# Queuing the steps that weigh batch 6's projections one product later

## The chip, the cores and the metric

The kernel runs on one core of a Trainium2 chip. The metric is the device time of one execution in microseconds (us), taken as the median of several runs. A core has engines with queues of their own: TensorE (PE, matrix products), VectorE (DVE), ScalarE (ACT), GpSimd (POOL) and SyncE (SP), which here only issues DMA transfers. Each engine takes its own instructions in order, and waits on semaphores for the others.

## The reference

The input x has 8 batches of 256 tokens with 1024 features, in float32. Every batch is first multiplied by one of eight 1024x1024 matrices, chosen by an index. The result, here called y, goes through a linear layer ("the base") and a mixture of eight low-rank updates:

```
y      = einsum('bsi,boi->bso', x, weight[ids])
base   = y @ base_W.T + base_b
probs  = softmax(y @ router_W.T + router_b)         # 15 choices per token
p, i   = top_k(probs, 8)
w      = sum of p by expert_map[i]                  # 8 experts
h      = einsum('btd,erd->bter', y, A)              # 8 experts x rank 16 = 128 values
lora   = einsum('bter,eor->bto', h * w, B) * 2
out    = x + base + lora
```

"Weighing the projections" is the product h * w for one batch, with the softmax, the choice of eight and the sum by expert that give w.

## The kernel before

**Two phases.** The first phase loops over the eight batches and computes y for each. It also projects a finished batch: `project(b, ph)` (line 129) multiplies y by the 128 columns of A and the 15 columns of the router at once (line 136). It returns six closures: `logits`, `softmax`, `top`, two of `route_to`, and `weigh`. `logits` reads the PSUM tile; the others work on small tiles in one large buffer named `late`; `weigh` multiplies h by w and transposes the result in 32x32 blocks through `flip` (line 244). `turn(b, hw)` (line 250) then makes 16 ScalarE copies (line 255) that put the blocks in place in `hwT0` or `hwT1`: the first holds batches 0 to 3, the second batches 4 to 7.

At the end of the first phase batch 6 is projected and its `logits` run; its other five closures are left in `steps`, which the second phase keeps as `steps_of` (line 568).

**The second phase** computes base and update for two groups of four batches (g = 0, 1). A group's 2x2 block product is itself written as seven outer products (`seven`, line 742), and each of them (`product`, line 597) again as seven blocks on PE, so that the base is done by a fast scheme in two levels. Counted over both groups, `here` numbers the outer products from 0 to 13; `n` counts within a group. A product works in three PSUM tiles:

- `pa`: a11 b11; then s2 t2 added; then s3 t3 added; then a22 t4 added
- `pc`: s1 t1; then s4 b22 added
- `pb`: a12 b21

In order the seven blocks are: `pa`, `pc`, `pa`, `pb`, `pa`, `pc`, `pa`. After each block, VectorE (or ScalarE where the base's bias is added, line 618) reads the tile as it stands: `take` copies it into the result quarter with a summand, `plus` adds it to a quarter (line 609). Since `pa` is added to in place, PE's next block into `pa` has to wait until the reader of the state before is done. Some products (n = 1, 3, 4, 6) also add the low-rank update to four of their blocks, by a matmul of the tiles `hwT` and `up` for each half (line 588); such a block takes PE longer.

**The order of the work is written out by hand** in this phase: PE, VectorE, ScalarE and SP take the instructions in the order in which the program issues them. Small VectorE work is fitted between the blocks through two queues, `soon` and `later`:

```
def fill(n):
    for _ in range(n):
        if soon or later:
            soon.popleft()() if soon else later.popleft()[1]()
```

Ahead of each of the seven blocks stands `gap(k)`, k = 0 to 6. It first runs the functions listed for that gap in `gaps[k]`, and then `fill(2)`. So the "third gap" is `gap(2)`, ahead of the block s2 t2. At the end of a product `fill(len(soon))` empties `soon` whatever its length, and `later` is worked off as far as it holds results of earlier quarters. What is queued in this way:

- the differences that the next product needs as its t1 to t4 (line 229; `advance`, put at the front of `soon`): two in gap 0, one in gap 3, one in gap 4
- the updates of y between the products (`first_terms` in product 0, `outer` in products 2 and 3; line 732)
- the residual add of x to a finished quarter and its output DMA (lines 703 and 704, in `later`)
- the weighing of batch 6 (`steps_of`) and of batch 7 (behind product 1)

After product 1 the kernel issues `turn` for batch 6 on ScalarE, projects batch 7 on PE and queues its steps; `turn` for batch 7 follows product 2.

DMA loads of the weights run through SP: `load_left` (line 206) fetches a product's seven block sums as two tiles, `left_raw` (line 209, 1024 KB) and `left_sum` (line 213, 768 KB). In gap 5 of a product those for the product after the next are issued. The quarters of x for the residual are loaded by `load_x` (line 694) in the gaps 0 to 3 of a product that ends in results. SP is a queue as well: a load that stands behind an output goes no earlier than that output.

Of the kernel before, what the change touches and what calls it, by code (L numbers as in the profile page):

```python
# [28 lines left out]
def kernel(  # L29
# [176 lines left out]
    def load_left(n):  # L206

        ra = wpool.tile([P, NS, 4 * P], F32, name="wt")
        nc.sync.dma_start(
            ra.rearrange("p s f -> p (s f)"), left_raw[n].rearrange("p s f -> p (s f)")  # L210
        )
        su = wpool.tile([P, NS, 3 * P], F32, name="wt")
        nc.sync.dma_start(
            su.rearrange("p s f -> p (s f)"), left_sum[n].rearrange("p s f -> p (s f)")
        )
        return ra, su

    def differences(right):

        b11, b12, b21, b22 = right[:, 0, 0], right[:, 0, 1], right[:, 1, 0], right[:, 1, 1]  # L220
        t = {}

        def minus(n, of, less):
            def run():
                t[n] = tpool.tile([P, 2 * S], F32, name="tt").rearrange(
                    "p (k o) -> p k o", k=2
                )
                x, y = (t[v] if isinstance(v, int) else v for v in (of, less))
                nc.vector.tensor_sub(t[n], x, y)
                return t[n]  # L230

            return run

        return [minus(1, b12, b11), minus(2, b22, 1), minus(3, b22, b12), minus(4, b21, 2)]
# [11 lines left out]
    def run(steps, n=None):  # L246
        for _ in range(len(steps) if n is None else min(n, len(steps))):
            steps.popleft()()

    def turn(b, hw):  # L250

        to = hwTs[b // GB][:, b % GB // 2, b % 2].rearrange("p (j a t) -> p j a t", j=NTT, a=4)
        return deque(
            (
                lambda a=a, r=r: nc.scalar.copy(  # L255
                    to[32 * r : 32 * r + 32, :, a, :],
                    hw[32 * a : 32 * a + 32, :, ts(r, 32)],
                )
            )
            for r in range(4)  # L260
            for a in range(4)
        )
# [282 lines left out]
    with ExitStack() as phase:  # L545
# [21 lines left out]
        soon, later = deque(), deque()  # L567
        steps_of = steps
# [110 lines left out]
        for g in range(B // GB):  # L679
            y, hw = yv[g], hwTs[g]  # L680
            end = g == B // GB - 1
            b11, b12, b21, b22 = y[:, 0, 0], y[:, 0, 1], y[:, 1, 0], y[:, 1, 1]
            u = mpool.tile([P, 2, 2, 2, S], F32, name="u")
            t2 = mpool.tile([P, 2, 2, 2, S], F32, name="t2")
            xs = {}

            def number(oh, th, i, j):
                return ((g * 2 + oh) * 2 + th) * 4 + 2 * i + j

            def load_x(*r):  # L690
                nonlocal loaded
                xs[r] = places_x[loaded % len(places_x)]
                loaded += 1
                nc.sync.dma_start(xs[r].rearrange("p m t -> p (m t)"), xr[number(*r)])

            def finish(oh, th):


                def done(i, j, q):
                    x, n = xs[oh, th, i, j], number(oh, th, i, j)  # L700

                    def run():
                        add(q, q, x)
                        nc.sync.dma_start(outq[n], q.rearrange("p m t -> p (m t)"))

                    later.append((q, run))

                return done

            def joint(i, j, q):  # L710


                def run():
                    add(q, v[:, i, j], q)

                soon.append(lambda: add(u[:, i, j], u[:, i, j], q))
                later.append((q, run))
                finish(1, 1)(i, j, q)

            def last(i, j, q):  # L720
                if (i, j) == (1, 0):
                    for mi in range(2):
                        nc.sync.dma_start(outq[number(1, 0, 1, 0), :, ts(mi, S)], q[:, mi])
                else:
                    finish(1, 0)(i, j, q)

            def at(t):
                return lambda i, j: t[:, i, j]

            def update(dst, x, z, quarters=((0, 0), (0, 1), (1, 0), (1, 1))):  # L730
                return [
                    (lambda i=i, j=j: sub(dst[:, i, j], x[:, i, j], z[:, i, j]))
                    for i, j in quarters
                ]

            def first_terms(*quarters):

                for q in quarters:
                    soon.extend(update(b11, b12, b11, [q]))
                    soon.extend(update(t2, b22, b11, [q]))  # L740

            seven = [

                (b11, 0, at(u), nothing),
                (b21, at(u), fresh, finish(0, 0), 0, hw[:, 0]),
                (t2, at(u), at(u), nothing),
                (b11, at(u), at(v), nothing, 1, hw[:, 1]),
                (b22, at(v), fresh, finish(0, 1), 2, hw[:, 1]),
                (b12, KH, fresh, joint),
                (b21, at(u), fresh, last if end else finish(1, 0), 1, hw[:, 0]),  # L750
            ]
            result_of = {1: (0, 0), 4: (0, 1), 5: (1, 1), 6: (1, 0)}

            outer = {2: update(b12, b22, b12), 3: update(b21, b21, t2)}

            for n, (right, base, into, done, *up_hw) in enumerate(seven):
                here = g * len(seven) + n
                gaps = {k: [] for k in range(7)}

                if n + 1 < len(seven):  # L760
                    follows = seven[n + 1][0]
                else:
                    follows = None if end else yv[g + 1][:, 0, 0]
                steps = [] if follows is None else differences(follows)
                nexts = []


                def advance(n, steps=steps, nexts=nexts):
                    def run():
                        soon.extendleft(  # L770
                            (lambda s=s: nexts.append(s())) for s in reversed(steps[n])
                        )

                    return run


                steps = [steps[:2], steps[2:3], steps[3:]]
                for k, m in ((0, 0), (3, 1), (4, 2)):
                    gaps[k].append(advance(m, steps))
                if n == 0:  # L780
                    gaps[1].append(lambda: first_terms((0, 0), (0, 1)))
                    gaps[4].append(lambda: first_terms((1, 0)))
                    gaps[6].append(lambda: first_terms((1, 1)))
                    if here == 0:
                        gaps[6].append(lambda: soon.extend(steps_of))
                elif n in outer:
                    gaps[1].append(lambda n=n: soon.extend(outer[n]))
                if n in result_of:
                    for k, ij in enumerate([(0, 0), (1, 1), (0, 1), (1, 0)]):
                        gaps[k].append(lambda r=result_of[n] + ij: load_x(*r))  # L790
                if end and n == 6:

                    r = (1, 0, 1, 0)
                    gaps[5].append(
                        lambda: soon.append(lambda: add(u[:, 1, 0], u[:, 1, 0], xs[r]))
                    )
                if here == 0:
                    for k, count in enumerate((0, 1, 1, 4, 4, 4, 2)):
                        gaps[k].append(lambda count=count: run(behind, count))
                if here + 2 < len(lefts):  # L800

                    def fetch(m=here + 2):
                        left[m] = load_left(lefts[m])

                    gaps[5].append(fetch)
                product(
                    left.pop(here), terms, right, base, into, done, gaps, *up_hw,
                    *([None] * (2 - len(up_hw))), end and n == 6
                )
                terms = nexts  # L810
                if here == 1:
                    run(turn(*waiting))

                    ph = ps_e.tile([P, 2, S], F32, name="pe")
                    steps, waiting = project(B - 1, ph)
                    soon.extend(steps)
                elif here == 2:
                    run(turn(*waiting))
# [65 lines left out]
```

## Time and profile before

| | |
|---|---|
| median of 3 runs | 435.79 us (435.49 to 436.15) |
| the profiled execution | 435.38 us |
| its span, first to last instruction | 433.6 us |
| TensorE busy | 426.8 us (98%) |
| VectorE busy | 328.9 us (76%) |
| ScalarE busy | 166.9 us (39%) |
| moved through DMA | 106.05 MB |

The span is what the profiler sees between the first and the last instruction; the time of the execution is a little longer. A busy share is an average over the span. In the rows of a timeline the first number is the start in us from the span's start, the second the duration, then engine, line, operation, and output <- inputs; a bracket gives the idle time before the row and what ended it. In the chain, the first number is the time at which a piece of the chain begins, the second how long it lasts. VectorE's rows may overlap a little: a row of 128x512 lasts 0.68 us and the next starts 0.60 us after it.

### The profile page before, as it was taken

To read this page: it belongs to the slowest core of one execution; us is meant where nothing else is said; L and a number is where in the kernel's file an instruction comes from. 1 tells how busy PE (TensorE), PEld (TensorE's weight loads), DVE (VectorE), ACT (ScalarE), POOL (GpSimd) and SP (SyncE) were. 2 spreads that over 40 slices of the span, in tenths; PEclk is the share of its full clock that TensorE was granted. 3 is DMA by queue.
4 is the path that set the end of the run, shared out by engine and by line. 5 is a ranking of instruction groups with operands and counts; after the bars stand their busy time and mean duration, and the time that the engine had idled before them with its cause. 6 is when DMAs were issued, how large, how long until landed. Compare 5 with 4: busy or idle time off the path is not lost.

```text
span 433.6 us, 4931 instructions
## 1 busy us (share of the span) xinstructions
PE 426.8 (98%) x1642; PEld 293.4 (68%) x1642; DVE 328.9 (76%) x556; ACT 166.9 (39%) x458; POOL 0.7 (0%) x6
## 2 busy tenths in 40 slices
PE   8999999999999999999999899999999999999997
PEld 5344554644646446454468798888888888888886
DVE  0799999986878898998786766946597858745595
ACT  1029287866659657686748500300201100000200
POOL 0000000000000000000000000000000000000000
PEclk9999999999999999999999999999999999999999
DMA  7996998968777797782859365522958725912843
GB/s 278 415 349 251 370 334 280 331 204 299 246 261 242 284 359 260 284 277 89 290 222 379 150 206 208 187 105 97 379 213 278 278 76 198 393 53 68 296 158 134
DMA packets 32779, 106.05 MB, mean 245 GB/s; under 512 B 3058, under 2 KB 6898, under 8 KB 29554
## 3 DMA queue, kind: packets, MB, share of 16 engines
q1 hardware_dynamic: 32610, 105.21, 66.8%
q10 hardware_dynamic: 144, 0.52, 0.3%
q8 instruction: 13, 0.21, 0.2%
q14 instruction: 12, 0.10, 0.1%
HBM read 84.49 MB, written 21.23 MB: 244 GB/s over the span
## 4 chain that ended last, share of the span: by engine, by line
PE 95%; DMA 2%; DVE 2%; SPq 1%; issue 0%; DVEq 0%
PE pa L290 24%; PE pa L579 21%; PE pc L290 13%; PE pc L579 11%; PE pb L290 7%; PE ph L136 6%; PE pb L579 6%; PE pc L588 3%; DMA wt<-in_wq_dram 2%; PE pb L588 2%; PE pa L588 1%; PE pe L136 1%; PE pe L579 1%; SPq L359 0%; DMA ids_sb<-in_ids_dram 0%
## 5 line engine op out<-in xcount | busy, mean ns | idle before, releaser
L308 ACT COPY y<-late 32x256 f32<-32x256 f32 x256 | 103.0, 402 | 41.9 <-DVE late L244 38.9
L579 PE MATMUL pa<-tt,wt 128*128 128x256 f32 x324 | 78.2, 380 | 1.6 <-DVE q L609 1.6
L579 PEld LDWEIGHTS pa<-tt,wt 128*128 128x128 f32 x324 | 61.2, 190 | 10.8 <-DVE q L609 2.0
L290 PE MATMUL pa<-wt,x 128*128 128x512 f32 x128 | 57.7, 593 | 0.4 <-DMA wt<-in_wq_dram 0.3
L290 PE MATMUL pa<-wt,tt 128*128 128x512 f32 x120 | 54.0, 593 | 0.0
L618 ACT ACTIVATE q<-pa,bb 128x256 f32<-128x256 f32 x12 | 5.0, 471 | 105.0 <-PE pa L579 104.0
L290 PEld LDWEIGHTS pa<-wt,x 128*128 128x128 f32 x128 | 24.2, 190 | 31.1 <-issue 30.2
L290 PEld LDWEIGHTS pa<-wt,tt 128*128 128x128 f32 x120 | 22.3, 190 | 26.2 <-issue 25.9
L255 ACT COPY hwT<-late 32x64 f32<-32x64 f32 x128 | 31.1, 243 | 10.6 <-DVE late L244 9.1
L136 PEld LDWEIGHTS ph<-late,y 128*128 128x128 f32 x224 | 28.4, 189 | 3.3 <-issue 3.3
L290 PE MATMUL pb<-wt,x 128*128 128x512 f32 x64 | 29.0, 594 | 0.4 <-DMA wt<-in_wq_dram 0.4
L290 PE MATMUL pc<-wt,x 128*128 128x512 f32 x64 | 28.9, 594 | 0.0
L290 PE MATMUL pc<-wt,tt 128*128 128x512 f32 x64 | 28.8, 592 | 0.0
L136 PE MATMUL ph<-late,y 128*128 128x143 f32 x224 | 28.6, 284 | 0.0
L579 PE MATMUL pc<-tt,wt 128*128 128x256 f32 x112 | 27.8, 379 | 0.0
L405 DVE TENSOR_TENSOR wt<-wt 128x2048 f32<-128x2048 f32 (+1 forms) x9 | 18.4, 2046 | 7.9 <-PE pa L290 5.5
L579 PE MATMUL pb<-y,wt 128*128 128x256 f32 x96 | 24.0, 379 | 0.0
L579 PE MATMUL pc<-y,wt 128*128 128x256 f32 x96 | 24.0, 379 | 0.0
L579 PEld LDWEIGHTS pc<-tt,wt 128*128 128x128 f32 x112 | 21.3, 190 | 2.9
L290 PEld LDWEIGHTS pb<-wt,x 128*128 128x128 f32 x64 | 12.1, 190 | 16.1 <-issue 14.3
L290 PEld LDWEIGHTS pc<-wt,x 128*128 128x128 f32 x64 | 12.1, 190 | 15.5 <-issue 14.8
L290 PEld LDWEIGHTS pc<-wt,tt 128*128 128x128 f32 x64 | 12.1, 190 | 15.3 <-issue 14.6
(118 smaller groups left out, 548.3 us busy)
## 6 DMA issues: line engine op xcount, KB each, us to landing
wt<-in_wq_dram SPq DMA_DIRECT2D x28, 1024.0 KB, 5.7
wt<-left_raw SPq DMA_DIRECT2D x14, 1024.0 KB, 5.7
wt<-left_sum SPq DMA_DIRECT2D x14, 768.0 KB, 7.6
out_dram<-q SPq DMA_DIRECT2D x31, 256.0 KB, 2.3
x<-in_xq_dram SPq DMA_DIRECT2D x7, 1024.0 KB, 6.9
late<-in_xr_dram SPq DMA_DIRECT2D x20, 256.0 KB, 6.6
wt<-in_wq_dram SPq DMA_DIRECT2D x8, 512.0 KB, 7.4
spare<-in_bq_dram SPq DMA_DIRECT2D x4, 1024.0 KB, 5.1
```

What stands on the lines that cost most here:

```text
L136: nc.tensor.matmul(ph[:, j, : ER + N], lhsT=y[:, k // KH, th, k % KH // 2, bi, k % 2, ts(j, P)], rhs=ar_sb[:, k, :], start=(j == order[0] ...
L255: lambda a=a, r=r: nc.scalar.copy(to[32 * r : 32 * r + 32, :, a, :], hw[32 * a : 32 * a + 32, :, ts(r, 32)],)
L290: nc.tensor.matmul(acc, lhsT=right[:, k, :], rhs=left[:, k, :], start=(first and k == 0), stop=(k == KH - 1), skip_group_check=True,)
L308: lambda a=a, r=r: nc.scalar.copy(y[32 * r : 32 * r + 32, :, :, a, :], m[32 * a : 32 * a + 32, :, :, r, :])
L405: nc.vector.tensor_add(q["s1"][:, h], q["a21"][:, h], q["a22"][:, h])
L579: nc.tensor.matmul(acc[mi][:, mi, :], lhsT=left[:, 2 * k + mi, :], rhs=right[:, k, :], start=(first and k == 0 and (mi == 0 or acc[0] is n ...
L588: nc.tensor.matmul(acc[mi][:, mi, :], lhsT=up[:, ts(mi, P)], rhs=hw, start=False, stop=True, skip_group_check=True,)
L618: nc.scalar.activation(dst[:, mi], acc[mi][:, mi], AF.Identity, bias=bb[:, c : c + 1])
```

## The change

The five closures left from batch 6 (`steps_of`) are appended to `soon` in gap 2 of outer product 1, where they were appended in gap 6 of outer product 0. In both kernels they are taken out by the same `fill`.

```diff
                     gaps[1].append(lambda: first_terms((0, 0), (0, 1)))
                     gaps[4].append(lambda: first_terms((1, 0)))
                     gaps[6].append(lambda: first_terms((1, 1)))
-                    if here == 0:
-                        gaps[6].append(lambda: soon.extend(steps_of))
                 elif n in outer:
                     gaps[1].append(lambda n=n: soon.extend(outer[n]))
+                if here == 1:
+                    gaps[2].append(lambda: soon.extend(steps_of))
                 if n in result_of:
```

The instructions of PE, ScalarE and GpSimd keep their order. On VectorE the rows from line 160 to the transpose of line 244, which stood together between the last update of y (line 732) and the first difference for product 2 (line 229), come apart:

- softmax and top (lines 160 to 179) stand behind the take of quarter (1,1) from `pc`, ahead of the take of (0,1) from `pa`
- the two route steps (lines 186 and 189) stand each behind one difference, ahead of the adds to (0,0) and to (1,1)
- the weighing and its transpose (lines 194 and 244) stand behind the add to (1,1), ahead of the first residual add

The residual adds from `later` come one place later as well: the first, ahead of the add to (1,1) before, now stands behind it; the second, ahead of the add to (0,1) before, now stands behind it. On SP the first output of product 1 follows the two weight loads of gap 5, where it stood ahead of them.

## The prediction

> **What bounds the kernel now.** I read the page first (shares and the chain), then who TensorE (PE) waited for, then the chain in order of time around the moved steps, then VectorE's (DVE) timeline there, last the DMA in stretches.
>
> ```profile
> span 433.6 us, 4931 instructions
> PE 426.8 (98%) x1642; PEld 293.4 (68%) x1642; DVE 328.9 (76%) x556; ACT 166.9 (39%) x458; POOL 0.7 (0%) x6
> PE 95%; DMA 2%; DVE 2%; SPq 1%; issue 0%; DVEq 0%
> ...
> PE pa L579 <- DVE q L609: 1.6, 1, 1.6
> PE pb L427 <- POOL ident masks.py:199: 1.4, 1, 1.4
> ```
>
> PE is busy for 426.8 of 433.6 us and is 95% of the chain that ended last. After the start-up it has one wait worth naming: once, 1.6 us, on the DVE instruction of line 609. The chain shows what stands in front of it:
>
> ```profile
> 236.34 1.74 PE pc L579 x8
> ...
> 240.19 0.10 DVE late L160
> ...
> 243.19 0.45 DVE late L244
> 243.64 0.59 DVE tt L229
> ...
> 244.93 0.69 DVE q L609
> 245.62 0.04 issue
> 245.66 1.99 PE pa L579 x8
> 247.66 0.86 PE pb L579 x4
> ```
>
> From 238.2 to 245.6 us the chain runs through DVE; everywhere else around here it runs through PE. The stretch 240.19 to 243.64 is exactly the moved steps (lines 160 to 244). DVE's timeline gives the order behind it:
>
> ```profile
> 240.11 0.18 DVE L160 TENSOR_REDUCE late<-late 128x2 f32<-128x30 f32 x1
> ...
> 243.19 0.45 DVE L244 STREAM_TRANSPOSE late<-late 128x256 f32<-128x256 f32 x1
> 243.56 0.65 DVE L229 TENSOR_TENSOR tt<-t 128x512 f32<-128x512 f32 x1
> 244.32 0.69 DVE L229 TENSOR_TENSOR tt<-t,tt 128x512 f32<-128x512 f32 x1
> 244.93 0.68 DVE L609 TENSOR_TENSOR q<-pa,u 128x512 f32<-128x512 f32 x1
> 245.53 0.68 DVE L609 TENSOR_TENSOR q<-pc,u 128x512 f32<-128x512 f32 x1
> 247.69 0.69 DVE L609 TENSOR_TENSOR q<-pa,u 128x512 f32<-128x512 f32 x1 [1.49 <-PE pa L579]
> ```
>
> The reader sees a queue: softmax to transpose, two differences, then the take of quarter (0,0) out of `pa`. PE's third block of product 1 accumulates into that same `pa` and may not start before the take has read it. PE's own rows have `pc` finished at 243.52 + 0.59 = 244.11 and the third block released at 245.66, just behind the take's end (244.93 + 0.68 = 245.61):
>
> ```profile
> 243.52 0.59 PE L588 MATMUL pc<-hwT,up 128*128 128x256 f32 x2
> 245.66 0.70 PE L579 MATMUL pa<-tt,wt 128*128 128x256 f32 x2 [1.55 <-DVE q L609]
> ```
>
> **The change part by part.**
>
> *Added and removed instructions:* none. Five closures (softmax, top, two route steps, weigh with its transpose) move on DVE from the end of product 0 into product 1. PE's and ScalarE's (ACT) orders stay as they are; on SyncE's (SP) queue one line trades places.
>
> *What leaves the end of product 0.* From the start at 240.11 to the start of the next row at 243.56: 3.45 us of DVE. With it gone, the differences start at 240.11 and 240.87 (0.76 apart, as now), and the take of (0,0) could start 0.61 later, at 241.48. But it also needs PE's first block, which starts at 239.63 and lasts 1.89: 241.52, plus the 0.04 that DVE needs after PE's end (247.65 to 247.69). So the take runs from 241.56 to 242.24. PE reaches its third block at 241.36 + 2.59 = 243.95 (2.59 is a block with the small rank-16 products: 247.66 to 250.25 in the chain). The take is 1.71 us early, so the wait is gone whole, not shortened.
>
> *What that is worth.* Idle time 1.55 (244.11 to 245.66), and the block that restarts costs 1.99 where one in the flow costs 1.73 in the chain: 0.26 more. Sum 1.81 us. The nearest rows bound it: at least 1.55 if the restart were paid anyway, at most the 1.95 that the weight loads sat idle. I take 1.81.
>
> *Where the 3.45 us go.* Each gap queues steps and runs two closures. Softmax and top run in the third gap, behind the take of `pc`; a difference and a route step in each of the fourth and fifth; weigh in the sixth. My timeline, PE without the wait, DVE pitches 0.60 for a 128x512 row:
> - PE: third block 243.95, `pb` 245.68, fifth block (`s3`) 248.27, `pc` again 250.00, last (`a22`) 252.59, projection of batch 7 from 255.18.
> - DVE: take of (1,1) from `pc` 244.15, then softmax and top (240.11 to 241.60: 1.49) from 244.75 to 246.24. Take of (0,1) out of `pa` starts 246.24; PE had it ready at 245.88. It is 0.36 late and ends at 246.92. PE's fifth block needs it at 248.27: 1.35 us spare.
> - Difference 246.84, route step (241.60 to 242.12: 0.52) to 247.97; `pb` is ready at 248.47, so the add to (0,0) is on time and ends 249.16. Difference 249.07, route step (0.62) to 250.29; the add of `pa` to (1,1) is ready at 250.20, so 0.09 late, done 250.97; PE's last block needs it at 252.59: 1.62 spare. (The two differences are read only in product 2.)
> - Weigh and transpose (242.74 to 243.56: 0.82) to about 251.7, one residual add to 252.3, the add of `pc` to (0,1) on time at 252.79. Two residual adds to 254.6; the take of (1,0) waits for PE at 255.38.
>
> So the 3.45 us fit into idle time that DVE has now: 1.49 before its row at 247.69, 1.30 before 250.28, 1.10 before 254.60 (idle on DVE in front of PE). Cost on the path: 0.
>
> *Who waits for the later transpose.* The 16 ACT copies of batch 6 (line 255) start at 243.67 now and would start near 251.8 and end near 256 (4.06 us). The next ACT work is the exponential of batch 7 at 264.16 now, some 262.4 then; 6 us of cover. These copies fill the half of `hwT1` that only the second group reads. The `hw0`, `w`, `kept` places are rewritten by batch 7's steps behind them on the same engine.
>
> *SP.* The residual add of (0,0) falls behind the sixth gap, so the two loads of the weights for product 3 (1024 + 768 KB) are queued ahead of its output, not behind it. They stand behind that output today and go at 252.65; they would go when SP is done with the x loads, at 233.61 + 0.92 = 234.5. The DMA engines are then nearly full:
>
> ```profile
> 236.00:240.00 4.00, 4.00 (x20) 3.54 (x19) 3.60 (x7) 3.65 (x10) 0.00 (x0) 1.00 0.99 413
> 240.00:244.00 4.00, 4.00 (x20) 3.27 (x18) 3.69 (x18) 0.99 (x4) 0.00 (x0) 1.00 0.67 253
> 244.00:248.00 4.00, 2.45 (x12) 2.08 (x12) 2.41 (x5) 3.57 (x15) 0.00 (x0) 1.00 0.00 0
> ```
>
> The transfers in flight end near 242.5; 1.83 MB more at 413 GB/s take 4.4 us, to 247, into a stretch that is empty now. Even if everything ended then, the x loads are first read at 251.5 and product 2's weights from 259.1. Cost 0, with 4.5 us of cover; the gain of earlier weights is 0 too, since PE never waits for them. The output of (0,0) goes out 0.2 us after its add, near 252.5; its tile is wanted again in product 4.
>
> *Sum.* The profiled execution took 435.38 us (span 433.6), 0.41 below the median 435.79. 435.38 - 1.81 = 433.57 for an execution like it; for a median of runs 435.79 - 1.81 = 433.98. From 245.66 on the chain is PE to the end, so the 1.81 us are not lost again unless one of the covers above fails.
>
> [...] By the rows, PE's blocks keep 1.73 us whatever DVE does, and DVE is busy 11.85 of 17.30 us between 239.8 and 257.1. [...]
>
> **The rivals.**
> 1. *The wait moves.* Softmax and top sit before the take of (0,1), the routes before the add to (1,1). If these run later than laid out by more than 1.35 or 1.62 us, PE's fifth or last block waits. For: the two are the only rows that my layout has late (0.36, 0.09). Against: all durations come from this very chain. With a wait of 0.3 to 0.9 us in place of 1.81: 434.3 to 434.9.
> 2. *DVE has no room:* the 3.45 us displace takes one for one and PE loses at the fifth and seventh blocks what it gained at the third. It would need the idle 1.49 + 1.30 + 1.10 not to be usable. Against: those rows wait for PE's results, not the reverse, and DVE is idle 5.45 of the 17.30 us. Same as before, 435.8. [...]
> 3. *Slower: the early weights.* 1.83 MB enter the DMA queue 18 us earlier, among x loads that take 10 us to land now. A residual add that waits for its x holds everything behind it on DVE: one more add, two residual adds, the take of (1,0), two differences, and then product 2's take of (0,0), seven rows of 0.60 to 0.76, some 4.5 us. PE reads past that take at product 2's third block, near 262.5, so it starts to cost once x lands after about 257.4, ten us behind the 247 above. To be slower than before by 0.9 it takes 257.4 + 1.8 + 0.9, near 260: 436.7. Against: they are issued ahead of the new loads.
>
> **How the numbers follow.** Forecast 0.86; rival 1 0.06; rival 2 0.05; rival 3 0.03. A measurement of this kernel tells about 0.2% (0.9 us) from no change. Half of rival 1 is faster by more than that. Faster 0.86 + 0.03 = 0.89; same 0.03 + 0.05 = 0.08; slower 0.03. The runs before spread from 435.49 to 436.15, so -0.30 and +0.36; the gain lies between 1.55 and 1.95. Low 435.49 - 1.95 = 433.5, high 436.15 - 1.55 = 434.6; I take 433.3 to 434.9, which takes in rival 1. The likeliest is 434.0.
>
> **What would show it.** Right: PE's line "waits for DVE q L609, 1.6" is gone; the span is near 431.8; the rows of lines 160 to 179 stand behind the take of `pc`, and the copies of line 255 start near 252; the weight loads for product 3 are issued near 234.5; PE idle between 240 and 257 is under 0.2. Wrong: a wait of PE on DVE at the fifth or last block of product 1, a wait on DMA in product 2, or a residual add (line 703) that waits for its x load.

## The result and the profile after

The changed kernel takes 434.02 us (median of 6 runs, 433.51 to 434.73) against 435.79 us (6 runs, 435.49 to 436.15): 0.9959 of the time before, 95% interval 0.9946 to 0.9972, that is 1.8 us less.

The page of the changed kernel, and from the list of whom TensorE waited for, all that is left:

```profile
span 432.3 us, 4927 instructions
PE 426.6 (99%) x1642; PEld 293.6 (68%) x1642; DVE 328.6 (76%) x556; ACT 167.0 (39%) x458; POOL 0.7 (0%) x6
PE 96%; DMA 2%; SPq 1%; issue 0%; DVE 0%
...
PE pb L427 <- POOL ident masks.py:199: 1.4, 1, 1.4
PE pb L290 <- DMA wt<-in_wq_dram: 1.0, 2, 0.6
PE pa L290 <- DMA wt<-in_wq_dram: 0.4, 1, 0.4
```

The wait of TensorE (PE) on the take of line 609 is gone. Busy times of PE and VectorE (DVE) are what they were, so no work went away. What is left are waits in the first microseconds, and these differ between profiled executions: 0.4 + 0.3 us on the first weights before, 1.0 + 0.4 here. Product 1 starts later in this profile, at 240.15 and not at 239.63. To compare the kernels I take the stretch from the start of product 1's first block to the end of the span: 433.6 - 239.63 = 193.97 before, 432.3 - 240.15 = 192.15 after, 1.82 us less. Both spans are given to 0.1 us, so such differences are good to about 0.1.

The chain of the changed kernel in order of time (start, length, what) runs through PE alone:

```profile
236.86 1.73 PE pc L579 x8
238.59 3.45 PE pa L579 x16
242.04 0.86 PE pc L579 x4
...
244.63 1.73 PE pa L579 x8
246.36 0.86 PE pb L579 x4
```

The third block, which cost 1.99 us behind a wait before, takes 1.73. VectorE's timeline in the same place:

```profile
240.63 0.68 DVE L229 TENSOR_TENSOR tt<-t 128x512 f32<-128x512 f32 x1
241.42 0.69 DVE L229 TENSOR_TENSOR tt<-t,tt 128x512 f32<-128x512 f32 x1
242.08 0.69 DVE L609 TENSOR_TENSOR q<-pa,u 128x512 f32<-128x512 f32 x1
244.67 0.69 DVE L609 TENSOR_TENSOR q<-pc,u 128x512 f32<-128x512 f32 x1 [1.90 <-PE pc L588]
245.28 0.17 DVE L160 TENSOR_REDUCE late<-late 128x2 f32<-128x30 f32 x1
...
246.54 0.19 DVE L179 TENSOR_TENSOR late<-late 128x30 f32<-128x30 f32 x1
246.65 0.68 DVE L609 TENSOR_TENSOR q<-pa,u 128x512 f32<-128x512 f32 x1
...
248.99 0.69 DVE L609 TENSOR_TENSOR q<-pb,q 128x512 f32<-128x512 f32 x1 [0.55 <-PE pb L588]
```

The take of (0,0) now starts when PE's first block is done, and PE reaches its third block 1.70 us after that take ends (242.77 to 244.47). VectorE then idles 1.90 us for `pc`, and only behind it come softmax and top. The take of (0,1) at 246.65 is the row that could become the next wait; it ends at 247.33, and PE wants it at 248.79, so its spare is 1.46 us.

### The profile page after: what moved, and what is told of

It is laid out like the page before. It is cut to its first block, busy times and chain, and to the rows that moved or that the text cites. A ratio compares the mean times of both kernels' runs of the same rounds, so it can differ in the third digit from the quotient of the medians.

```text
span 432.3 us, 4927 instructions
## 1 busy us (share of the span) xinstructions
PE 426.6 (99%) x1642; PEld 293.6 (68%) x1642; DVE 328.6 (76%) x556; ACT 167.0 (39%) x458; POOL 0.7 (0%) x6
## 4 chain that ended last, share of the span: by engine, by line
PE 96%; DMA 2%; SPq 1%; issue 0%; DVE 0%
PE pa L290 24%; PE pa L579 22%; PE pc L290 13%; PE pc L579 11%; PE pb L290 7%; PE ph L136 6%; PE pb L579 6%; PE pc L588 3%; DMA wt<-in_wq_dram 2%; PE pb L588 2%; PE pa L588 1%; PE pe L136 1%; PE pe L579 1%; SPq L359 0%; DMA ids_sb<-in_ids_dram 0%
```

## The experiments

Each was compared with the kernel before on the same chip, which took 435.57 us beside the first four kernels, 435.80 beside the next four and 435.70 beside the last. "Stretch" is product 1's start to the end of the span, as above.

**How much may stay ahead of the take of (0,0)?** Two kernels put a part of the steps back at the end of product 0.

```diff
+                    if here == 0:
+                        gaps[6].append(lambda: soon.extend(steps_of[:2]))
...
-                    gaps[2].append(lambda: soon.extend(steps_of))
+                    gaps[2].append(lambda: soon.extend(steps_of[2:]))
```

> Softmax and top (1.49 us of VectorE) go back to the end of product 0, the other 1.96 us of the 3.45 stay in product 1. Threshold theory: the take of (0,0) has 1.7 us to spare in the changed kernel, 1.49 fits, so TensorE still does not wait at the third block of product 1 and the median is that of the changed kernel, 434.0 (product 1's start to the end 192.15 us). Rival, each microsecond ahead of the take costs its share: 434.0 + 1.81 * 1.49/3.45 = 434.8.

Measured: 433.91 us (433.67 to 434.31), ratio 0.9963 (0.9949 to 0.9976); stretch 432.5 - 240.35 = 192.15, the same as the changed kernel's. PE has no wait. The first row of softmax, and the rows up to the take of (0,0) and the one behind it:

```profile
240.83 0.17 DVE L160 TENSOR_REDUCE late<-late 128x2 f32<-128x30 f32 x1
...
242.20 0.68 DVE L229 TENSOR_TENSOR tt<-t 128x512 f32<-128x512 f32 x1
242.99 0.69 DVE L229 TENSOR_TENSOR tt<-t,tt 128x512 f32<-128x512 f32 x1
243.60 0.69 DVE L609 TENSOR_TENSOR q<-pa,u 128x512 f32<-128x512 f32 x1
244.87 0.69 DVE L609 TENSOR_TENSOR q<-pc,u 128x512 f32<-128x512 f32 x1 [0.58 <-PE pc L588]
```

The take of (0,0) ends at 244.29, 0.38 us before PE is due at 240.35 + 4.32 = 244.67. The proportional theory (434.8) falls.

With `[:4]` and `[4:]` in place of `[:2]` and `[2:]`:

> All but the weighing and its transpose go back: 3.45 - 0.82 = 2.63 us ahead of the take of (0,0). Threshold theory: the take ends 0.82 earlier than before, at product 1's start + 5.16; TensorE wants it at + 4.32, so a wait of about 0.73 and a restart 0.26 dearer, about 1.0 us over the changed kernel: 435.0. Rival, proportional: 434.0 + 1.81 * 2.63/3.45 = 435.4.

Measured: 434.76 us (434.31 to 435.88), ratio 0.9984 (0.9975 to 0.9993); stretch 432.9 - 239.87 = 193.03, 0.88 over the changed kernel. From VectorE's timeline, then PE's:

```profile
240.35 0.18 DVE L160 TENSOR_REDUCE late<-late 128x2 f32<-128x30 f32 x1
...
242.86 0.68 DVE L229 TENSOR_TENSOR tt<-t 128x512 f32<-128x512 f32 x1
...
244.25 0.69 DVE L609 TENSOR_TENSOR q<-pa,u 128x512 f32<-128x512 f32 x1
```

```profile
239.87 1.89 PE L579 MATMUL pa<-y,wt 128*128 128x256 f32 x8
...
244.99 1.99 PE L579 MATMUL pa<-tt,wt 128*128 128x256 f32 x8 [0.64 <-DVE q L609]
```

The wait is back with 0.64 us, in its old place. So the cost is a threshold. With 1.37 us of the steps ahead (240.83 to 242.20) nothing is lost, with 2.51 us (240.35 to 242.86) 0.88, with the 3.45 us of the kernel before 1.82: between the last two, 0.94 us more of the steps costs 0.94 us more. The threshold itself lies near the spare of 1.70 us; no kernel was run just above it. The restarted block is 0.1 dearer in its own length again (1.99, not 1.89).

**Is there room behind it?** Softmax and top, whose results do not change when they are repeated, run twice or three times in the third gap.

```diff
-                    gaps[2].append(lambda: soon.extend(steps_of))
+                    gaps[2].append(
+                        lambda: soon.extend(
+                            [lambda: [s() for s in steps_of[:2] * 1 + steps_of[:1]]] + steps_of[1:]
+                        )
+                    )
```

(`* 2` for three times.)

> The changed kernel with softmax and top done twice over in the third gap of product 1: 1.49 us more of VectorE ahead of the take of (0,1). In the changed kernel that take ends 1.46 us before TensorE's fifth block needs it. Theory (there is room up to that spare): 0.0 to 0.3 us over the changed kernel, 434.0 to 434.3. Rival (VectorE is the bound, no room): 1.49 over it, 435.5.

Measured: 434.35 us (433.77 to 435.07), ratio 0.9971 (0.9959 to 0.9983); stretch 432.7 - 240.48 = 192.22, 0.07 over. PE shows no wait. The median lies 0.05 above the range that I expected; the runs spread over 1.3 us, so I go by the stretch.

> Softmax and top three times in the third gap: 2.98 us more. Theory: the spare of 1.46 is used up, a wait of TensorE on the take of (0,1) of about 1.5 us at the fifth block appears, with its restart 1.6 to 1.8 us over the changed kernel, 435.7. Rival (no room): 2.98 over it, 437.0.

Measured: 435.26 us (435.12 to 435.94), ratio 0.9993 (0.9984 to 1.0002); stretch 433.9 - 240.27 = 193.63, 1.48 over. The takes of (0,1) with twice and with three times the steps, and PE's fifth block behind the second, each from the timeline of its kernel:

```profile
248.25 0.19 DVE L179 TENSOR_TENSOR late<-late 128x30 f32<-128x30 f32 x1
248.36 0.69 DVE L609 TENSOR_TENSOR q<-pa,u 128x512 f32<-128x512 f32 x1
```

```profile
249.52 0.69 DVE L609 TENSOR_TENSOR q<-pa,u 128x512 f32<-128x512 f32 x1
...
250.26 1.99 PE L579 MATMUL pa<-tt,wt 128*128 128x256 f32 x8 [1.20 <-DVE q L609]
```

Twice: the take ends at 249.05, and PE's block starts at 249.12, just when it is due (240.48 + 8.64). Three times: the take ends at 250.21 where PE was due at 248.91, and the wait appears at the fifth block, where rival 1 of the prediction puts it. VectorE had just one more softmax and top of room, as the spare said. Each repeat is 1.37 us (245.61 to 246.98), not the 1.49 that I took, and so the cost is 1.48 and not 1.6 to 1.8.

**Does VectorE's work in product 1 cost anything?** The five steps of batch 6 are left out.

```diff
-                if here == 1:
-                    gaps[2].append(lambda: soon.extend(steps_of))
```

> The changed kernel without the softmax, choice, sum by expert and weighing of batch 6 (its update then uses values left by batch 4): 3.45 us of VectorE less in product 1. Theory (the steps are fully covered in their new place): no change against the changed kernel, 434.0, within 0.1 us in the trace from product 1's start to the end (192.15). Rival (VectorE's occupancy sets the time): up to 3.45 us less, 430.6.

Measured: 434.04 us (433.68 to 434.07), ratio 0.9954 (0.9941 to 0.9968); stretch 432.2 - 240.08 = 192.12. The busy columns of the stretch 239.8 to 255.3 (PE, weight loads, VectorE, ScalarE), first without the steps:

```profile
239.80:255.30 15.50, 15.50 (x74) 13.64 (x73) 9.31 (x15) 4.82 (x19) 0.00 (x0) 1.00 0.45 164
```

and in the changed kernel:

```profile
239.80:255.30 15.50, 15.50 (x74) 13.64 (x73) 12.05 (x31) 4.05 (x15) 0.00 (x0) 1.00 0.55 220
```

2.74 us of VectorE less and 0.03 us of time: in their new place the steps cost nothing. (The 3.45 us of the expectation are the length of the chain as it stood before; the columns count busy time in the new place.) PE is busy for all 15.50 us in both. Without the steps ScalarE makes its 16 copies from 241.01 on, in the changed kernel from 252.25 on, and the stretch is the same: their later place is not the gain either.

**The weight loads.** The change also sends two loads of product 3's weights ahead of product 1's first output. One kernel does that alone, in the kernel before; another undoes it alone, in the changed kernel.

```diff
-                    gaps[5].append(fetch)
+                    gaps[4 if here == 1 else 5].append(fetch)
```

> The kernel before with one part of the change alone: the two weight loads for product 3 are queued on SP ahead of product 1's first output, so they go some 18 us earlier; the weighing stays where it was. Theory: no effect, 435.8 (product 1's start to the end 193.97). Rival, the earlier weights bring part of the gain: 434.0 to 435.3. Rival, they cost something that the change hides: over 436.2.

Measured: 435.69 us (435.48 to 436.07), ratio 0.9999 (0.9990 to 1.0008); stretch 434.0 - 240.01 = 193.99. PE's wait stays as it was:

```profile
246.04 1.99 PE L579 MATMUL pa<-tt,wt 128*128 128x256 f32 x8 [1.55 <-DVE q L609]
```

```diff
-                    gaps[5].append(fetch)
+                    gaps[6 if here == 1 else 5].append(fetch)
```

> The changed kernel with those two loads behind product 1's first output, as before. Theory: no effect, 434.0 (192.15). Rival, the earlier weights are part of the gain: up to 435.3.

Measured: 433.96 us (433.41 to 434.37), ratio 0.9956 (0.9942 to 0.9969); stretch 432.2 - 240.03 = 192.17. SyncE's timeline of the changed kernel, then of this one:

```profile
234.63 0.91 SPq L694 DMA_DIRECT2D late<-in_xr_dram  x2
236.23 0.33 SPq L209 DMA_DIRECT2D wt<-left_raw  x1
238.12 0.33 SPq L213 DMA_DIRECT2D wt<-left_sum  x1
252.82 2.74 SPq L704 DMA_DIRECT2D out_dram<-q  x3
```

```profile
252.70 0.34 SPq L704 DMA_DIRECT2D out_dram<-q  x1
253.14 0.38 SPq L209 DMA_DIRECT2D wt<-left_raw  x1
253.61 0.41 SPq L213 DMA_DIRECT2D wt<-left_sum  x1
```

The loads move by 15 to 17 us either way, and nothing follows. Of the change, VectorE's order is what is left as the cause.

**Another place.** The steps are queued one gap earlier, still behind the take of (0,0).

```diff
-                    gaps[2].append(lambda: soon.extend(steps_of))
+                    gaps[1].append(lambda: soon.extend(steps_of))
```

> The changed kernel with the five steps queued one gap earlier, in the second gap of product 1: softmax and top then run while VectorE waits for the block in pc, and the take of (0,1) is on time. Theory (any place behind the take of (0,0) with enough spare is equal): 434.0 (192.15), with the take of (1,1) on time or under 0.1 late. Rival, the lateness of takes costs even without a wait of TensorE: 0.2 to 0.4 us faster than the changed kernel.

Measured: 433.95 us (433.75 to 434.21), ratio 0.9956 (0.9943 to 0.9970); stretch 432.0 - 239.80 = 192.20. From VectorE's timeline:

```profile
243.61 0.19 DVE L179 TENSOR_TENSOR late<-late 128x30 f32<-128x30 f32 x1
244.32 0.69 DVE L609 TENSOR_TENSOR q<-pc,u 128x512 f32<-128x512 f32 x1 [0.52 <-PE pc L588]
...
246.05 0.69 DVE L609 TENSOR_TENSOR q<-pa,u 128x512 f32<-128x512 f32 x1
```

Softmax and top fill most of the wait for `pc`, and the take behind them still waits 0.52 us for PE. The take of (0,1) at 246.05 starts as soon as PE's third block is done (239.80 + 4.32 + 1.89 = 246.01), where it was 0.25 us late in the changed kernel (246.65 against 246.40). No time comes of it: a late take that PE does not wait for costs nothing.

**What is left in product 2.** In the changed kernel VectorE holds PE's weight loads once more, ahead of product 2's last block, and that block takes 1.99 us:

```profile
270.04 1.59 PEld L579 LDWEIGHTS pa<-tt,wt 128*128 128x128 f32 x8 [0.31 <-DVE u L609]
270.05 1.99 PE L579 MATMUL pa<-tt,wt 128*128 128x256 f32 x8
```

Here it is the weighing of batch 7, ahead of the add to (1,1), as VectorE's timeline shows:

```profile
268.97 0.45 DVE L244 STREAM_TRANSPOSE late<-late 128x256 f32<-128x256 f32 x1
269.34 0.65 DVE L609 TENSOR_TENSOR u<-pa,u 128x512 f32<-128x512 f32 x1
```

One kernel runs two more closures in the first gap of product 2:

```diff
+                elif here == 2:
+                    gaps[0].append(lambda: fill(2))
```

> The changed kernel with two more closures run in the first gap of product 2, so that batch 7's logits and softmax come ahead of the take of (0,0), in VectorE's idle 3.56 us, and its weighing ahead of the take of (0,1), not ahead of the add to (1,1). In the changed kernel TensorE starts the last block of product 2 at 270.05, 0.07 after the 269.98 of an unbroken flow, and that block costs 0.10 more. Theory (the same reading holds here): the add to (1,1) is on time, the stretch from product 1's start to the end goes from 192.15 to 191.98, the median to 433.85, less than a measurement can tell. Rival (moving it only shifts the wait to the third or fifth block of product 2): 192.15 or more.

Measured: 433.53 us (433.38 to 433.97), ratio 0.9956 (0.9942 to 0.9971); stretch 431.6 - 239.65 = 191.95. Its PE timeline:

```profile
259.11 1.89 PE L579 MATMUL pa<-t,wt 128*128 128x256 f32 x8
...
269.47 1.95 PE L579 MATMUL pa<-tt,wt 128*128 128x256 f32 x8
271.25 1.89 PE L579 MATMUL pa<-y,wt 128*128 128x256 f32 x8
```

and the rows of VectorE that matter there:

```profile
268.08 0.68 DVE L732 TENSOR_TENSOR y<-y 128x512 f32<-128x512 f32 x1
268.68 0.68 DVE L609 TENSOR_TENSOR u<-pa,u 128x512 f32<-128x512 f32 x1
```

Product 2 takes 271.25 - 259.11 = 12.14 us where the changed kernel takes 271.88 - 259.62 = 12.26. The last block starts in the flow, but is still 0.06 dear: the add to (1,1) was not on time as I had expected, because two updates of y (line 732, at 266.29 and 268.08) moved up in front of it; it starts at 268.68 where PE's block was done at 267.90, and ends 0.11 us before PE's last block, whose weight loads it holds for 0.19 us. The 0.12 us can be read in the trace; the medians can't tell this kernel from the changed one.

## Why the prediction was right

**The wait and its price.** I gave 1.55 us of idle time and 0.26 for the restart, 1.81; the stretch shrank by 1.82, and the median by 1.77. That the median came within 0.04 us of the 433.98 is luck, as the runs spread from 433.51 to 434.73; the stretch and the rows are what bear the forecast out. Of the 0.26, 0.16 is the overlap with the block before (blocks last 1.89 and start 1.73 apart), 0.10 the longer block. That the restart counts is shown by the kernel with four steps back, too: PE waited 0.64 us there and lost 0.88.

**The timeline.** Taken from product 1's start (0.52 later in this profile), the rows lie where the prediction put them:

| | predicted | measured - 0.52 |
|---|---|---|
| take of (0,0) | 241.56 | 241.56 |
| PE's third block | 243.95 | 243.95 |
| take of (0,1) | 246.24 | 246.13 |
| add to (1,1) | 250.29 | 250.19 |
| first ScalarE copy of batch 6 | 251.8 | 251.73 |
| PE's last block | 252.59 | 252.58 |

**One term was mis-sized,** the length of softmax and top: 1.49 us by the start of the route step behind them, 1.37 by the row that follows now (245.28 to 246.65). The spare at the fifth block is 1.46, not 1.35. It mattered in the experiments with repeats and not in the forecast. The span came out at 432.3 and not near 431.8, because product 1 started 0.52 us later in this execution.

**The covers.** The ScalarE copies started at 252.25 and ended near 256.3; the exponential of batch 7 came at 262.87. The loads went at 236.2 and 238.1, not at 234.5: the loads of x ended at 235.54, and SyncE then held the weights 0.6 and 1.5 us for earlier loads. The DMA was empty again by 248 (share 0.87 from 244 to 248, 0.02 from 248 to 252), near the 247 of the forecast, and no residual add waited for its x. One reason given for the cover was wrong and harmless: batch 7's steps do not rewrite `hw0`, since line 145 gives them `hw1`.

**The rivals.** The wait did not move (1), though two more rounds of softmax and top move it to the very block that was named. VectorE had room (2). The Trainium skill (Perfetto Trace Analysis, Identifying the Most-Contended Engine) would rank VectorE, at 76% occupancy, above PE with 68% by weight loads, one of its two signs for PE. That is over the whole span; here 2.74 us less of VectorE's work gave 0.03 us, and the order of the same work gave 1.82. Over the 15.50 us around product 1 alone, as shown above, weight loads take 13.64 us and VectorE 12.05, so the same ranking puts PE first: a share of the span averages over stages with different limits. The early loads (3) cost nothing, alone or with the rest.

## What to carry to other kernels

An accumulator that is added to in place makes its reader a gate: before fitting side work between blocks, note for each reader when its input is ready and when the next writer is due, and put ahead of it only as much side work as its spare holds. The cost of side work ahead of such a gate is a threshold, nothing up to the spare, then the price of the restart and microsecond for microsecond, so neither its length nor the engine's busy share tells what moving it is worth. To test a spare, repeat the harmless part of the work until the wait comes back.

## What the runs showed of the hardware

- A VectorE row that does not read the result of the row ahead starts sooner. Among rows of 128x512, the second difference, which reads the first, started 0.79 us after it (240.63 to 241.42 after the change); rows that read nothing of the row ahead start 0.60 apart (246.65 to 247.25). Behind line 179 the dependent route step started 0.22 us after it (241.38 to 241.60 before), the independent take 0.11 us after it (246.54 to 246.65), with 0.08 of the older row still to run. The same chain of small rows is therefore shorter where an independent row follows. The Trainium skill (VectorE: DVE Perf Modes, The DRAIN you can't avoid) says that the next operation starts only when the pipe is empty, but also that one that is not held starts earlier; the independent take, which started with 0.08 us of the row ahead still to run, agrees with the latter.
- A block of PE that restarts behind a wait lasts 1.99 us, not 1.89, after waits of 1.55, 1.20 and 0.64 us alike, at a granted clock of 1.00. The last block of product 2 in the changed kernel lasts 1.99 us too, where only its weight loads had sat idle, for 0.31 us; after 0.19 us in the kernel with batch 7 earlier it is 1.95. What makes the block longer is not shown.
- Product 1 started anywhere from 239.63 to 240.48 in the eleven profiles, though PE's work up to there is the same; the waits for the first weights vary (0.5 to 1.5 us in all). That is half a gain of this size, and the reason to compare stretches of the trace.
